# Deformable sampling on one core: where ScalarE's copy of turned samples stands in its slot

## The chip, the core and the metric

The kernel runs on one core of one Trainium2 chip. The metric is the device time of one execution in microseconds (us), the median of several. The core has TensorE (matrix products, "PE" in the profile), VectorE ("DVE"), ScalarE ("ACT"), GpSimd ("POOL"), SyncE ("SP") and DMA queues. Each engine runs its own list of instructions in order and waits on semaphores for the others.

## What is computed

Two layers work on an image of shape (4, 256, 64, 64). What matters here is layer 0. It normalizes `x` over the channels, derives 18 offsets and 9 masks for each pixel from a 3 x 3 convolution, samples the normalized image at nine shifted places for each pixel, and convolves the samples:

```python
val = ((1-wy)*(1-wx))[..., None]*corner(y0i, x0i) + ((1-wy)*wx)[..., None]*corner(y0i, x1i) \
    + (wy*(1-wx))[..., None]*corner(y1i, x0i) + (wy*wx)[..., None]*corner(y1i, x1i)
val = val * mask[..., None]
out = jnp.einsum('bkhwc,ock->bohw', val, w_conv.reshape(O, C, K))
```

Then x = x + out, and a recurrence with gates runs over the 4096 pixels of each image:

```python
i_t = sigmoid(xi_t + h @ V_i); g_t = tanh(xg_t + h @ V_c); o_t = sigmoid(xo_t + h @ V_o)
c_new = h * c + i_t * g_t
h_new = o_t * tanh(c_new)
```

Layer 1 has a gate for each channel from statistics of the whole image, and a second recurrence of the same kind.

## The kernel before, in words

The 16384 pixels lie in 128 tiles of 128 pixels by 256 channels. Each image is cut into 32 segments of 128 steps, which run beside each other on the 128 partitions; 16 warm-up steps guess each segment's start, so the first recurrence has 144 steps.

The kernel has three stretches. The first (to about 200 us) normalizes the input, writes a table of 2 x 2 pixel squares to DRAM and works out the sampling plan (`prepare`). The second, about 207 to 2290 us and the one that matters here, is `sample_and_recur` (line 577): it samples and convolves layer 0, and beside that runs the first recurrence behind the sampled tiles, and gathers the statistics for layer 1. The recurrence goes on for a short time when the sampling is done. The third is `gated_lstm`, the second recurrence.

The unit of sampling is a pair: two of the 128 x 9 combinations of tile and tap, so 576 pairs (`PAIRS`, line 601). A pair goes through six steps:

- `gather` (line 623): POOL issues two indirect DMAs, 512 KB each, that bring for each pixel its square of four corners (`squares`). There is room for five pairs.
- `scale` (line 645): ACT multiplies the first corner of each of the two by its weight and writes `v` (two activations of 128 x 256). `v` has six buffers, so three pairs.
- `combine` (line 652): DVE adds the other three corners with their weights to `v`, six instructions.
- `turn` (line 658): PE transposes the two `v` into PSUM (`tr`, two buffers).
- `copy` (line 665): ACT copies `tr` to SBUF as `vt`, one instruction of 128 x 512 (three buffers).
- `convolve` (line 672): PE multiplies `vt` with the convolution's weights and adds up in PSUM (`acc`).

The loop over slots `s` at lines 1066 to 1100 writes the order of the work out by hand, and the class `InOrder` (line 396) ties each engine's instructions to it; line 425, which the profile shows for nearly everything, is its wrapper's. In slot s the pairs stand at these steps: ACT copies pair s-2 and scales pair s+1; DVE combines pair s; PE convolves pair s-3 and, at the end of its slot, turns pair s-1; POOL gathers pair s+5. Engines run their slots independently, bound only by their waits.

A step of the recurrence comes every 4.5 slots (`step_slot`, line 926). `core` (line 987) spreads it over slots counted from `at` = 0: PE's products with h for two gates (`ga`) at 0 and for the third (`gb`) at 1; ACT's tanh and sigmoid for `tg` and `ti` at 1, `to` and `th` at 2 (`gates_of`, line 959); DVE's `cell` at 1 and `h` at 2; PE's products of the next step's input (`ga`, `gb`) at 2 and 3. Spare work (normalization, statistics, `nm`, `sq`, `xn`, `y`, `lanes`) is put behind these in each slot by `fill` (line 1047) from a list of tasks with assumed costs.

So ACT's list in slot s was: copy of pair s-2, gates if the slot has any, scaling of pair s+1, spare work.

Of the kernel before, what the change touches and what calls it, by code (L numbers as in the profile page):

```python
# [496 lines left out]
def recur(nc, G, Vs, h, shared=SHARED):  # L497

    for gs in shared:
        for g in gs:  # L500
            for m in range(NC):
                for k in range(NC):
                    nc.tensor.matmul(
                        G[g][:, m],
                        Vs[:, k, g, m * P : (m + 1) * P],
                        h[:, k],
                        start=False,
                        stop=(g == gs[-1] and m == NC - 1 and k == NC - 1),
                        skip_group_check=True,
                    )  # L510
# [30 lines left out]
def shift(nc, to, guess):  # L541

    to, guess = segments(to), segments(guess)
    nc.vector.memset(to[:, :, :, 0:1], 0.0)
    nc.vector.tensor_copy(to[:, :, :, 1:R], guess[:, :, :, 0 : R - 1])


class Spare:
# [6 lines left out]
    def give(self, engine, slot, us, do, room=lambda: True, urgent=False, soon=False):  # L555
        left = self.todo.setdefault(engine, [])
        at = 0 if urgent else sum(t[4] for t in left) if soon else len(left)
        left.insert(at, (slot, us, do, room, urgent or soon))
# [18 lines left out]
def sample_and_recur(  # L577
# [23 lines left out]
    PAIRS = NTILE * K // 2  # L601
# [43 lines left out]
    def scale(n):  # L645
        r = rounds[n]
        for i in range(2):
            v = vp.tile([P, C], F32, name="v", tag="v", bufs=6)
            nc.scalar.activation(v, r["sq"][i][:, 0:C], AF.Copy, scale=r["w"][i][0])
            r["v"].append(v)  # L650
# [43 lines left out]
    def fetch(p):  # L694

        n = 2 * p
        assert n < RING or {n - RING, n - RING + 1} <= through
        nc.sync.dma_start(place(n, 2), (x_in if n in SAMPLED else x1)[:, ORDER[n] : ORDER[n] + 2])
# [133 lines left out]
    now, free = {"slot": 0}, [*range(SQUARES)]  # L832
    taken = {"xn": 0, "y": 0, "ms": 0, "ys": 0, "cm": 0}

    def room(tag, n):
        return lambda: free if tag == "y" and now["slot"] > PAIRS + 16 else taken[tag] < n
# [89 lines left out]
    def step_slot(n):  # L926
        return START + (9 * n) // 2
# [15 lines left out]
    def project_part(n, gs):  # L943
        cm = cms[n - n % 2][:, n % 2]

        other = n % 2 and step_slot(n) > PAIRS + 8
        if gs == SHARED[0]:
            at, tag = (ps_ac, "acc") if other else (ps_a, "ga")
            ga = at.tile([P, 2, NC, P], F32, name="ga", tag=tag)
            G[n] = {gs[0]: ga[:, 0], gs[1]: ga[:, 1]}  # L950
        else:
            at, tag = (ps_tr, "tr") if other else (ps_b, "gb")
            G[n][gs[0]] = at.tile([P, NC, P], F32, name="gb", tag=tag)
        project(nc, G[n], Us, cm, (gs,))
        if gs == SHARED[1] and n % 2:
            del cms[n - 1]
            taken["cm"] -= 1

    def gates_of(n, gs):
        for g, f in gs:  # L960
            name = {2: "tg", 0: "ti", 1: "to"}[g]
            state[name] = st.tile(shape, F32, name=name, tag=name)
            for m in range(NC):
                nc.scalar.activation(state[name][:, m], G[n][g][:, m], f, bias=bs[:, g, m : m + 1])

    def added(n, slot):

        h = state.pop(("h", n))
        taken["ms"] += 1
        ht = ps_ms.tile([P, C], F32, name="ht", tag="ms")  # L970
        for k in range(NC):
            nc.tensor.transpose(ht[:, k * P : (k + 1) * P], h[:, k], ident)

        def add(slot):
            b, j = divmod(n, NB)
            plus(place(n)[:, 0], ht, b + 2, NB + j)
            taken["ms"] -= 1
            if n % 2:
                nc.sync.dma_start(x2[:, ORDER[n] - 1 : ORDER[n] + 1], place(n - 1, 2))
            if n >= LAST:  # L980
                spread(n, 1, b + 2, NB + j, slot)
            else:
                give("ACT", slot + 1, 0.9, lambda s: spread(n, 1, b + 2, NB + j, s))

        give("DVE", slot + 1, 0.48, add, urgent=n >= LAST)

    def core(s, engine):

        us = 0.0
        for n in sorted({max(0, (2 * (s - START - d)) // 9 + e) for d in range(5) for e in (0, 1)}):  # L990
            if not FIRST <= n < STEPS:
                continue
            at = s - step_slot(n)
            if engine == "PE":
                if n == FIRST and at in (-2, -1):
                    project_part(FIRST, SHARED[at + 2])
                    us += 1.8 if at == -2 else 0.9
                if at == 0 and n > FIRST:
                    recur(nc, G[n], Vs, state["h"], (SHARED[0],))
                    us += 1.8  # L1000
                if at == 1 and n > FIRST:
                    recur(nc, G[n], Vs, state["h"], (SHARED[1],))
                    us += 0.9
                if at in (2, 3) and n + 1 < STEPS:
                    project_part(n + 1, SHARED[at - 2])
                    us += 1.8 if at == 2 else 0.9
                if at == 3 and n >= WARM:
                    give("PE", s, 0.22, lambda slot, n=n: added(n, slot), room("ms", 1))
            if engine == "ACT":
                if at == 1:  # L1010
                    gates_of(n, ((2, AF.Tanh), (0, AF.Sigmoid)))
                    us += 1.0
                if at == 2:
                    gates_of(n, ((1, AF.Sigmoid),))
                    state["th"] = st.tile(shape, F32, name="th", tag="th")
                    nc.scalar.activation(state["th"], state["c"], AF.Tanh)
                    us += 0.9
            if engine == "DVE":
                if at == 1:
                    nc.vector.tensor_mul(state["tg"], state["tg"], state["ti"])  # L1020
                    nc.vector.tensor_add(state["c"], state["hc"], state["tg"])
                    us += 0.86
                if at == 2:
                    h = state["hguess"] if n == WARM - 1 else st.tile(shape, F32, name="h", tag="h", bufs=3)
                    nc.vector.tensor_mul(h, state["to"], state["th"])
                    if n >= WARM:
                        state["h", n] = h
                    if n == WARM - 1:
                        h = st.tile(shape, F32, name="h", tag="h", bufs=3)
                        shift(nc, h, state["hguess"])  # L1030
                        shift(nc, state["cell"], state["cguess"])
                        state["c"] = state["cell"]
                    state["h"] = h
                    if n + 1 < STEPS:
                        state["hc"] = st.tile(shape, F32, name="hc", tag="hc")
                        nc.vector.tensor_mul(state["hc"], h, state["c"])
                    us += 0.86
        return us
# [26 lines left out]
    s = 0  # L1065
    while s <= step_slot(STEPS) or not spare.empty():
        if s % 9 == 0 and s // 9 + 2 + FIRST // 2 <= STEPS // 2 - 1:
            p = s // 9 + 2 + FIRST // 2
            fetch(p)
            if 2 * p not in SAMPLED:  # L1070
                b, q = divmod(2 * p, NB)
                give(
                    "ACT",
                    s + 32,
                    0.9,
                    lambda slot, b=b, q=q // 2: normed(b, q, *normal[b - NTILE // NB], slot),
                    room("xn", 2),
                )
        if s > PAIRS + 16 and errands:
            errands.pop(0)(nc)  # L1080
        if 0 <= s - 2 < PAIRS:
            copy(s - 2)
        now["slot"] = s
        us = core(s, "ACT")
        if s + 1 < PAIRS:
            scale(s + 1)
        fill("ACT", s, us)
        if s < PAIRS:
            combine(s)
        fill("DVE", s, core(s, "DVE"))  # L1090
        if 0 <= s - 3 < PAIRS:
            convolve(s - 3, s)
        fill("PE", s, core(s, "PE"))
        if 0 <= s - 1 < PAIRS:
            turn(s - 1)
        if s + AHEAD < PAIRS:
            gather(s + AHEAD)
        s += 1
# [830 lines left out]
```

## Time and profile before

| | |
|---|---|
| median of 20 executions | 3220.79 us (3199.28 to 3239.57) |
| the profiled execution | 3202.81 us, of which the profile's span is 3200.9 us |
| mean granted clock of TensorE | 0.978 |
| copies `vt` from `tr`: 576, 206.8 to 2282.1 us | 336.3 us busy, 584 ns each; ACT idle ahead of them 672.4 us |
| scalings `v` from `squares`: 1152 | 527.9 us busy, 513 ns each; ACT idle ahead of them 41.2 us |
| PE in 1300 to 1600 us | 289.5 of 300 us busy |
| DVE in 1300 to 1600 us | 270.4 of 300 us busy |
| ACT in 1300 to 1600 us | 198.6 of 300 us busy |

The profile is one execution, followed by the hardware. A group is a line, an engine, an operation and the tiles that it writes and reads ("vt<-tr"). "Idle before" is the time in which the engine had nothing to run ahead of an instruction, with the engine whose release ended it. PE's starts are measured, the ends of its products modelled. In a timeline each row gives the start, the busy time, the engine, the operation, the tiles, the number of merged instructions and, in brackets, the idle time ahead and its releaser. Idle time of an engine is a loss only where the engine that sets the pace waits for it.

### The profile page before, as it was taken

What the parts mean: (1) busy time and instruction counts of PE and PEld (TensorE: products, weight loads), DVE (VectorE), ACT (ScalarE), POOL (GpSimd) and SP (SyncE); (2) the same over time, 40 slices, a digit from 0 to 9 for tenths busy, and PEclk for the clock granted to TensorE, in tenths of its full rate; (3) what the DMA queues carried; (4) which work ended last, traced back from release to release, by engine and by line L of the source; (5) the groups of instructions that cost most, each with busy time, mean ns of one, the idle gap of its engine ahead of it and who ended that gap; (6) DMA issues with size and microseconds to landing.
All of it is one profiled execution on the core that took longest, in us unless ns stands there. A gap on an engine that the chain in (4) does not pass through costs nothing.

```text
span 3200.9 us, 61683 instructions
## 1 busy us (share of the span) xinstructions
PE 3029.4 (95%) x20252; PEld 2809.6 (88%) x20252; DVE 2668.8 (83%) x7864; ACT 2043.9 (64%) x5414; POOL 1578.3 (49%) x1595
## 2 busy tenths in 40 slices
PE   7958999999999999999999999999996999999998
PEld 6947889998999889998889989999995999999997
DVE  6757778888899899998899989999777777777774
ACT  6734556666667667676676767777775666666663
POOL 3356556666666666665666656666200122222221
PEclk9979999999999999999999999999998999999999
DMA  9988788988898889998989898999401144444442
GB/s 314 326 297 332 285 287 319 329 310 317 306 334 312 310 305 331 320 322 309 330 303 329 313 318 307 333 316 327 163 27 60 60 150 151 143 151 150 150 138 87
DMA packets 319065, 822.04 MB, mean 257 GB/s; under 512 B 100872, under 2 KB 106504, under 8 KB 316432
## 3 DMA queue, kind: packets, MB, share of 16 engines
q0 software_dynamic: 189312, 672.57, 59.9%
q1 hardware_dynamic: 128992, 144.82, 13.3%
q8 instruction: 163, 2.67, 0.3%
q14 instruction: 166, 1.36, 0.1%
q10 hardware_dynamic: 432, 0.63, 0.1%
HBM read 697.98 MB, written 119.89 MB: 256 GB/s over the span
## 4 chain that ended last, share of the span: by engine, by line
PE 86%; DMA 4%; DVE 3%; ACT 3%; issue 2%; another core or an unknown queue 1%; POOL 0%; SPq 0%; ACTq 0%; DVEq 0%
PE acc L425 30%; PE ga L425 15%; PE tr L425 8%; PE gacc L425 7%; PE gtr L425 7%; PE gb L425 7%; PE gga L425 4%; PE ggb L425 4%; DMA table<-ring 2%; PE xt L425 1%; PE ht L425 1%; DMA squares<-table,used 1%; ACT v L425 1%; DMA Us<-in_L_ffn_U_c_dram 1%
## 5 line engine op out<-in xcount | busy, mean ns | idle before, releaser
L425 POOL DMA_INDIRECT squares<-table,used x1152 | 1324.1, 1149 | 755.7 <-DVE v L425 164.1
L425 DVE SCALAR_TENSOR_TENSOR v<-squares,used,v 128x256 f32<-128x256 f32 x3456 | 1413.7, 476 | 107.1 <-ACT v L425 77.7
L425 PE MATMUL acc<-wconv,vt 128*128 128x256 f32 x4608 | 1113.9, 385 | 60.5 <-ACT vt L425 38.0
L425 PEld LDWEIGHTS acc<-wconv,vt 128*128 128x128 f32 x4608 | 842.0, 193 | 166.7 <-ACT vt L425 47.2
L425 ACT COPY vt<-tr 128x512 f32<-128x512 f32 x576 | 336.3, 584 | 672.4 <-PE tr L425 529.8
L425 ACT ACTIVATE v<-squares,used 128x256 f32<-128x256 f32 x1152 | 527.9, 513 | 41.2 <-DMA squares<-table,used 36.8
L425 PE MATMUL tr<-ident,v 128*128 128x128 f32 x2304 | 350.8, 274 | 30.5 <-DVE v L425 25.4
L425 PEld LDWEIGHTS tr<-ident,v 128*128 128x128 f32 x2304 | 275.2, 142 | 42.9 <-DVE v L425 22.8
L425 PEld LDWEIGHTS ga<-cm,Us 128*128 128x128 f32 x2240 | 272.9, 193 | 8.4 <-issue 1.1
L425 PEld LDWEIGHTS ga<-h,Vs 128*128 128x128 f32 x2224 | 271.1, 193 | 6.4
L425 PE MATMUL ga<-cm,Us 128*128 128x128 f32 x2240 | 275.1, 276 | 1.4 <-issue 1.1
L425 PE MATMUL ga<-h,Vs 128*128 128x128 f32 x2224 | 273.0, 276 | 0.0
L425 DVE TENSOR_TENSOR tg<-tg,ti 128x256 f32<-128x256 f32 x280 | 118.2, 422 | 144.6 <-ACT ti L425 135.5
L425 POOL DMA_DIRECT2D hd<-sqh x60 | 35.0, 583 | 387.5 <-DVE sqh L425 325.2
L425 POOL DMA_DIRECT2D ring<-hd x240 | 144.8, 632 | 161.3 <-DMA hd<-sqh 155.1
L425 DVE TENSOR_TENSOR h<-to,th 128x256 f32<-128x256 f32 x278 | 117.1, 421 | 123.7 <-ACT th L425 119.1
L425 ACT ACTIVATE tg<-gacc,bs 128x128 f32<-128x128 f32 x280 | 87.7, 364 | 174.2 <-PE gacc L425 174.2
L425 PEld LDWEIGHTS gb<-cm,Us 128*128 128x128 f32 x1120 | 147.6, 192 | 18.0 <-issue 11.5
L425 PE MATMUL gb<-cm,Us 128*128 128x128 f32 x1120 | 152.3, 276 | 8.1 <-issue 7.7
L425 PEld LDWEIGHTS gb<-h,Vs 128*128 128x128 f32 x1112 | 145.8, 193 | 8.8 <-issue 2.4
L425 PEld LDWEIGHTS gacc<-h,Vs 128*128 128x128 f32 x1112 | 144.0, 191 | 10.0 <-DVE h L425 3.2
L425 PE MATMUL gb<-h,Vs 128*128 128x128 f32 x1112 | 148.0, 276 | 2.2 <-issue 2.2
(226 smaller groups left out, 4608.0 us busy)
## 6 DMA issues: line engine op xcount, KB each, us to landing
squares<-table,used POOLq DMA_INDIRECT x1152
ring<-in_x_dram SPq DMA_DIRECT2D x65, 256.0 KB
x1d<-ring SPq DMA_DIRECT2D x64, 256.0 KB
x2d<-ring SPq DMA_DIRECT2D x64, 256.0 KB
ring<-x2d SPq DMA_DIRECT2D x16, 1024.0 KB
out_dram<-ring SPq DMA_DIRECT2D x32, 512.0 KB
hd<-sqh POOLq DMA_DIRECT2D x60, 256.0 KB
ring<-hd POOLq DMA_DIRECT2D x240, 64.0 KB
```

Of the source, the lines that this page charges most:

```text
L425: ins = op(*args, **kw)
```

## The change

In the loop over slots, ACT now scales pair s+1 first, then works the gates if the slot has any, and then copies pair s-2; before, it copied, worked the gates and then scaled. Spare work stays last. The lists of PE, DVE, POOL and SP are the same as before.

```diff
         if s > PAIRS + 16 and errands:
             errands.pop(0)(nc)
+        now["slot"] = s
+        if s + 1 < PAIRS:
+            scale(s + 1)
+        us = core(s, "ACT")
         if 0 <= s - 2 < PAIRS:
             copy(s - 2)
-        now["slot"] = s
-        us = core(s, "ACT")
-        if s + 1 < PAIRS:
-            scale(s + 1)
         fill("ACT", s, us)
         if s < PAIRS:
             combine(s)
```

## The prediction

> **What bounds the kernel now.** I read the busy times of the whole span first. TensorE (PE) is busy 3029.4 of 3200.9 us. The sampling stretch, which the change touches, runs from the first to the last copy of turned samples, 206.8 to 2282.1 us. I then read the waits in that stretch, longest total first, and last the timeline of one stall.
>
> ```profile
> PE 3029.4 (95%) x20252; PEld 2809.6 (88%) x20252; DVE 2668.8 (83%) x7864; ACT 2043.9 (64%) x5414; POOL 1578.3 (49%) x1595
> ```
>
> ```profile
> ACT vt L425 <- PE tr L425: 529.8, 339, 7.0
> ...
> DVE v L425 <- ACT v L425: 64.3, 28, 5.1
> ...
> DVE tg L425 <- ACT ti L425: 40.1, 36, 6.3
> PE acc L425 <- ACT vt L425: 38.0, 30, 4.0
> ```
>
> The columns are total us, times, longest. ScalarE (ACT) stands idle 529.8 us ahead of its copies (vt from tr) for PE's transposes, which costs nothing by itself. What costs is the last line: 30 times PE had nothing to do until a copy was done. Those 38.0 us are the largest item of PE idle time there. From 440 to 2290 us PE's groups show 35.6 us idle ahead of the convolution (28.7 of it for copies), 8.1 ahead of gb, and 4.3 ahead of tr, ga and xt: 48.0 us in 1850. VectorE's lateness does not reach PE: "PE tr <- DVE v" is 25.4 us in two waits, 22.6 of them in one at the ramp. So PE sets the pace, and it can gain at most about 48 us here.
>
> One of the 30 waits:
>
> ```profile
> 1495.14 0.60 PE L425 MATMUL tr<-ident,v 128*128 128x128 f32 x4
> ...
> 1495.58 1.89 PE L425 MATMUL acc<-wconv,vt 128*128 128x256 f32 x8
> ...
> 1498.78 0.79 PE L425 MATMUL tr<-ident,v 128*128 128x128 f32 x4
> ...
> 1500.70 0.59 ACT L425 COPY vt<-tr 128x512 f32<-128x512 f32 x1 [6.55 <-PE tr L425]
> 1501.18 0.91 ACT L425 ACTIVATE v<-squares,used 128x256 f32<-128x256 f32 x2
> ...
> 1501.34 1.99 PE L425 MATMUL acc<-wconv,vt 128*128 128x256 f32 x8 [1.77 <-ACT vt L425]
> 1501.72 2.47 DVE L425 SCALAR_TENSOR_TENSOR v<-squares,used,v 128x256 f32<-128x256 f32 x6 [3.63 <-ACT v L425]
> ```
>
> The transposes end at 1495.74 by the trace, but ACT sees their release only at 1500.70. At once it copies; the convolution follows 0.05 us behind the copy's end, and the two scalings come behind the copy, for VectorE (DVE). The DMA share in 1495 to 1501 is 1.00 at 379 GB/s. Why the release is late I can't tell from this; what matters is what stands between it and PE. Before it is only the copy.
>
> **What the change does, part by part.** In slot s, ACT's order was copy(s-2), gates, scale(s+1), spare work. It becomes scale(s+1), gates, copy(s-2), spare work. Nothing is added or removed: 576 copies, 1152 scalings and the gate activations stay, and the lists of the other engines and queues (PE, DVE, POOL's gathers, SP's DMAs) do not change. Only one wait moves. `v` has 6 buffers, two for a slot, so scale(s+1) writes the buffers that turn(s-2) reads. Before, the copy ahead of it had waited for that turn; now each scaling carries a wait for PE itself, and the copy none. So scalings do not escape the wait on the transposes: they take it over, and gates and copy stay behind it.
>
> *What comes earlier.* (1) The scalings, by the copy, 0.48 us from its start to the next instruction's (1500.70 to 1501.18), and in the two slots of each step of the recurrence by the gates, about 1.0 us. They serve DVE, which PE does not wait for; I cost this at nothing. What hides it is PE's own queue, 97% full here. If that cover is gone, this is the faster rival below.
>
> *What comes later.* (2) The gates: they stood behind one copy (0.48 us) and now stand behind two scalings (0.66 to 0.88 us, worked out in 3), so about 0.3 us later. DVE waits 36 times for `ti`, so it may idle 36 x 0.3 = 11 us more. What hides it: PE's products with h show 0.0 us idle ahead (ga from h, 273.0 us busy). I cost it at 0; without cover it is 11.
>
> (3) The copy, by two scalings, and in 227 of 511 slots by the gates as well. A pair of scalings takes 0.91 us; the next instruction starts 0.81 to 0.88 us behind the first (1501.18 to 1501.99). The first scaling needs only the first half of the transposes, released up to 0.22 us ahead of the second. So the shift is 0.66 to 0.88 us; I take 0.75, the middle. With gates it is 1.0 more, 1.75 (tg to v in the group's rows: 1312.04 to 1313.06). Who waits for the copy: PE at convolve(s-2), in the next slot, and behind it everything on PE. Cover is the time from the copy's end to that matmul. I took it pair by pair from the trace after 440 us (the last three pairs, which have no scaling ahead, left out):
> - 39 pairs have under 0.15 us. 12 of them follow directly on another, with ACT idle for under 0.5 us, and share its shift, so 27 count once, 19 without gates and 8 with: 19 x 0.75 + 8 x 1.75 = 28 us (26 to 32 with 0.66 and 0.88).
> - Of the others without gates, 17 have 0.15 to 1.0 us (mean 0.52): those below the shift lose 5 us together. With gates, 27 have 0.15 to 1.8 us (mean 1.29): 27 x (1.75 - 1.24) = 14, less 0.05 of each cover being the semaphore's way. Together 19; but many of these are late because of a stall just before, whose shift they share. I take 10 (0 to 25).
> - The rest have cover to spare: without gates 2.7 us in the median of all, with gates 2.3, against shifts of 0.75 and 1.75.
>
> (4) The ramp, 207 to 440 us, 62 pairs. 13 of these have under 0.15 us of cover, but gathers limit there ("ACT v <- DMA squares" 20.1 us, and 22.6 us on DVE at once), and a copy behind a scaling that waits for its gather is late by that wait. Each by 0.75 would be 10 and with gates in 3 of them 13, with longer gather waits some 20, hidden 0. I take 4, nearer the hidden end, as PE is not the bound there. After the ramp gathers do not matter: no wait of ACT for a gather is listed between 700 and 2200 us.
>
> (5) The clock. After long PE waits the granted clock halves:
>
> ```profile
> 440.00:444.50 4.50, 2.97 (x8) 2.34 (x8) 2.05 (x6) 3.49 (x9) 0.00 (x0) 0.62 0.72 292
> ...
> 1915.00:1925.00 10.00, 7.70 (x34) 6.86 (x35) 6.37 (x16) 6.17 (x19) 2.15 (x2) 0.66 0.63 236
> ```
>
> The columns are stretch, us, busy time of PE, PEld, DVE, ACT, POOL, then the granted clock. At 0.62 over 4.5 us, 1.7 us of full clock are lost, at 0.66 over 10 us 3.4. Between 440 and 2290 us this happens five times (441, 820, 1342, 1762, 1916), beside PE waits of 1.5, 1.8, 3.0, 1.8 and 4.0 us; 13 waits there are of 1.5 us or more, so not each brings it. With waits 0.75 to 1.75 us longer I take two or three more such stretches: 4 us. The ends are 0 (none more) and 41 (24 stretches of 1.7 us, one for nearly every one of the 27).
>
> The Trainium skill, "TensorE: Matmul & The Clock Gate", section "HAM oscillation — how this bites in real kernels", has PE go back to the slow clock for idle gaps over about 3.4 us; by that rule waits of 1.8 + 0.75 us would bring no stretch more, term 5 would be 0 and the sum 42. The trace differs: three of the five fell beside waits of 1.5 to 1.8 us. I go by the trace.
>
> Sum: 28 + 10 + 4 + 4 = 46 us more. The profiled execution took 3202.81 us (span 3200.9 and 1.9 around it); with the change it would take some 3249. It lies 18 us under the median of the 20 runs, 3220.79, so for the median I put 3220.8 + 46 = 3267.
>
> **Rivals.**
>
> *It makes no difference (0.15).* The late releases may mostly not stand on the path: the modelled end of PE's work may hide that PE is still busy while its queue looks empty, so that a copy 0.75 us later meets a PE that was not idle. Then only the second item of term 3 is left, some 0 to 10 us, less what DVE gains: about 3224. For it: the profile gives PE's ends as modelled. Against it: a queue that is really idle is what lets the clock fall, and it falls beside these waits.
>
> *Faster (0.20).* DVE gets scaled samples 0.5 to 1.5 us earlier. DVE idles 64.3 us for `v`, 40.1 for `ti`, 34.0 for `th` in the stretch. POOL's gathers are issued on DVE's releases (164.1 us of POOL's waits), so late scalings bunch gathers, and the stall above came in a stretch of full DMA. If the late releases come of this bunching, steadier gathers would thin them out. With half of PE's 38.0 us of copy waits gone and the rest of DVE's gain hidden, that is -19: 3202. The most is -48, all PE idle. It decides if more of the 27 waits vanish than the added 0.75 or 1.75 us on those left is worth. Against it: gathers are issued some 11 us ahead of their use, and moving a scaling by 0.5 to 1.5 us in a slot of 3.5 us changes little in when DMA is full.
>
> *Much slower (0.10).* The clock falls with nearly every lengthened wait: 24 x 1.7 = 41 in place of 4, so 46 + 37 = 83, 3304. It needs waits of some 2.5 us to trigger where those of 1.7 mostly did not.
>
> *It doesn't do what it says* is no case of its own: the copies do move, and that the scalings keep a wait on PE is in the sum.
>
> **How the numbers follow.** My forecast, 3267, has 0.55. Its own range is 3247 to 3306: the low ends of the terms sum to 26; the high ends, with 8 for the clock, to 32 + 25 + 20 + 8 = 85. For 8 in 10 I reach down to 3202, which leaves out half of the faster case, and up to 3300, which leaves out half of the much slower one. Faster by over 0.2% (6.4 us, about what a measurement of this kernel can tell from no change) 0.20; within it 0.15; slower 0.65.
>
> **What would show it.** Right: "PE acc <- ACT vt" grows from 38.0 us by 30 to 50, single waits of some 1.7 become 2.4 and more; idle ahead of ACT's copies falls to nearly nothing and reappears ahead of `v` (from PE tr); DVE's waits for `v` shrink, those for `ti` grow; PE idle rises though DVE idles less in their stead. The stretch from 2290 us on keeps its length. Wrong: PE's waits for copies become fewer than 20, or stay at 1.7 with the copy still directly behind the release; or the stretch after 2290 us changes; or PE begins to wait for DVE.

## The result and the profile after

The changed kernel takes **3264.15 us** in the median of 9 runs (3250.97 to 3275.22); the kernel before, run beside it on the same chip, 3219.36 (62 runs). The ratio is 1.014, with a 95% interval of 1.0117 to 1.0164: 45 us slower. The profiled execution of the changed kernel took 3280.24 us, 16 above its median, that of the kernel before 3202.81, 17 under its own. So the two traces lie 77 us apart, the medians 45, and a size read from the traces is too large for the medians.

The busy times of the whole span, from the page of the changed kernel:

```profile
PE 3057.5 (93%) x20252; PEld 2829.2 (86%) x20252; DVE 2668.6 (81%) x7864; ACT 2046.7 (62%) x5414; POOL 1592.0 (49%) x1595
```

DVE's busy time is that of before and ACT's nearly so: nothing was added. PE's grew by 28 us in the same 20252 matmuls, so some of them ran at a lower clock.

Now the waits in the stretch of sampling, 207 to 2380 us (total us, times, longest):

```profile
ACT v L425 <- PE tr L425: 522.7, 356, 6.7
...
PE acc L425 <- ACT vt L425: 82.0, 35, 6.2
DVE tg L425 <- ACT ti L425: 75.6, 38, 6.6
...
PE tr L425 <- DVE v L425: 29.8, 2, 27.6
...
DVE v L425 <- ACT v L425: 24.0, 20, 6.5
```

The first line was "ACT vt" before, 529.8 us: the wait on PE's transposes has gone from the copy to the scaling, as large as it was. DVE's wait for `v` fell from 64.3 to 24.0, that for `ti` rose from 40.1 to 75.6. PE's wait for copies rose from 38.0 to 82.0. The groups of the page say the same of the two instructions that changed places (busy, mean ns, then the idle time ahead and the releaser of most of it). The copy before:

```profile
L425 ACT COPY vt<-tr 128x512 f32<-128x512 f32 x576 | 336.3, 584 | 672.4 <-PE tr L425 529.8
```

The scaling and the copy after:

```profile
L425 ACT ACTIVATE v<-squares,used 128x256 f32<-128x256 f32 x1152 | 529.9, 503 | 800.0 <-PE tr L425 522.7
...
L425 ACT COPY vt<-tr 128x512 f32<-128x512 f32 x576 | 331.7, 576 | 1.0 <-PE tr L425 1.0
```

The copy now hardly ever waits (672.4 us of idle time ahead of it before, 1.0 after), because the scaling ahead of it already has.

Where the time came from shows in three stretches, parted at the first copy and the last: ramp (62 pairs), rest of the sampling, tail. The columns are us, then the busy times of PE, PEld, DVE, ACT and POOL, the granted clock, DMA share and GB/s:

```profile
213.70:455.30 241.60, 204.16 (x1174) 181.87 (x1175) 177.37 (x501) 118.14 (x298) 148.25 (x127) 0.90 0.83 296
455.30:2359.80 1904.50, 1820.56 (x12068) 1686.42 (x12067) 1682.01 (x4841) 1244.77 (x3319) 1179.03 (x1014) 0.98 0.86 305
2359.80:3278.30 918.50, 870.11 (x6046) 812.36 (x6044) 676.15 (x2003) 565.60 (x1560) 180.52 (x304) 0.97 0.36 114
```

In the trace of before the same stretches take 234.2, 1841.1 and 918.8 us, with PE busy for 203.6, 1794.1 and 870.5; the middle one reads:

```profile
441.00:2282.10 1841.10, 1794.05 (x12056) 1668.34 (x12057) 1681.75 (x4840) 1241.46 (x3320) 1164.08 (x1012) 0.99 0.89 315
```

So of the 77 us, 6.9 came ahead of the first copy, in code that is the same (206.8 to 213.7 us), 7.4 in the ramp, 63.4 in the rest, and none in the tail. The 63.4 are 36.9 us more of PE idle time (47.1 to 83.9) and 26.5 us more of PE busy time in as many matmuls. The second is the clock: by the trace's records of it, five stretches of half clock before in this part, losing 10.2 us, and sixteen after, losing 35.8.

One late release in the changed kernel (start, busy time, engine, tiles):

```profile
1397.62 0.60 PE L425 MATMUL tr<-ident,v 128*128 128x128 f32 x4
...
1403.50 0.51 ACT L425 ACTIVATE v<-squares,used 128x256 f32<-128x256 f32 x1 [7.30 <-remote]
1404.91 0.51 ACT L425 ACTIVATE v<-squares,used 128x256 f32<-128x256 f32 x1 [0.90 <-remote]
1405.32 0.60 ACT L425 ACTIVATE tg<-ga,bs 128x128 f32<-128x128 f32 x2
1405.82 0.62 ACT L425 ACTIVATE ti<-ga,bs 128x128 f32<-128x128 f32 x2
1406.32 0.60 ACT L425 COPY vt<-tr 128x512 f32<-128x512 f32 x1
1406.47 0.42 DVE L425 TENSOR_TENSOR tg<-tg,ti 128x256 f32<-128x256 f32 x1 [6.55 <-ACT ti L425]
...
1406.97 2.50 PE L425 MATMUL acc<-wconv,vt 128*128 128x256 f32 x5 [5.69 <-ACT vt L425]
```

The transposes end at 1398.22, and ACT goes on only at 1403.50 and, for the second half, at 1404.91 (the profile does not name the releaser here, only "remote"). The copy starts 1.41 us behind that, after a scaling and two pairs of gates; PE stood idle for 5.69 us, in which DVE waited for the same gates. Before, the copy stood directly behind such a release. The windows view of what follows:

```profile
1404.20:1411.00 6.80, 4.03 (x11) 3.31 (x12) 4.46 (x12) 5.08 (x14) 0.93 (x1) 0.50 0.63 254
```

The granted clock is 0.50 for 6.8 us: another 3.4 us lost, seen as longer busy times and not as idle time.

### The profile page after: what moved, and what is told of

The parts are those of the page before. It is cut to its first block, busy times and chain, and to the rows that moved or that the text cites. A ratio compares the mean times of both kernels' runs of the same rounds, so it can differ in the third digit from the quotient of the medians.

```text
span 3278.3 us, 62133 instructions
## 1 busy us (share of the span) xinstructions
PE 3057.5 (93%) x20252; PEld 2829.2 (86%) x20252; DVE 2668.6 (81%) x7864; ACT 2046.7 (62%) x5414; POOL 1592.0 (49%) x1595
## 4 chain that ended last, share of the span: by engine, by line
PE 74%; issue 12%; DVE 5%; ACT 4%; another core or an unknown queue 3%; DMA 2%; POOL 0%; SPq 0%; ACTq 0%; DVEq 0%; POOLq 0%
PE acc L425 26%; PE ga L425 12%; PE tr L425 7%; PE gacc L425 6%; PE gtr L425 6%; PE gb L425 6%; PE ggb L425 3%; PE gga L425 3%; DVE v L425 3%; ACT v L425 1%; ACT vt L425 1%; PE zacc L425 1%; PE xt L425 1%; DMA table<-ring 1%
## 5 line engine op out<-in xcount | busy, mean ns | idle before, releaser
L425 POOL DMA_INDIRECT squares<-table,used x1152 | 1338.6, 1162 | 812.9 <-DVE v L425 240.3
L425 PE MATMUL acc<-wconv,vt 128*128 128x256 f32 x4608 | 1134.5, 390 | 109.8 <-ACT vt L425 82.0
L425 PEld LDWEIGHTS acc<-wconv,vt 128*128 128x128 f32 x4608 | 852.8, 195 | 225.8 <-ACT vt L425 94.0
L425 ACT ACTIVATE v<-squares,used 128x256 f32<-128x256 f32 x1152 | 529.9, 503 | 800.0 <-PE tr L425 522.7
L425 PE MATMUL ga<-cm,Us 128*128 128x128 f32 x2240 | 282.7, 278 | 8.9 <-issue 8.2
L425 PE MATMUL gacc<-h,Vs 128*128 128x128 f32 x1112 | 147.0, 275 | 1.8 <-DVE h L425 1.8
```

The costliest lines, as they stand in the source:

```text
L425: ins = op(*args, **kw)
```

## The experiments

My theory: a copy that comes later costs only where a release from PE reaches ACT late, and there PE pays for all that ACT works between release and copy, and for the clock. The rivals: the order costs by itself; the later gates cost, through DVE; the number or the length of the late releases itself changes with the order.

The kernels ran on three chips, each beside the kernel before on the same chip: its median there was 3189.44 us (the first four kernels), on the second chip 3093.05 (the next four) and in a second set 3095.60 (three more), on the third 3208.36 (the last). The chips differ by more than the change makes, and that became a finding. Of the kernel before a trace was kept on the chip of the first comparison alone, so figures of waits "before" are from there, and against traces of another chip they are a rough measure.

**Half of the change: scaling first, then copy, then gates.**

```diff
+        now["slot"] = s
+        if s + 1 < PAIRS:
+            scale(s + 1)
         if 0 <= s - 2 < PAIRS:
             copy(s - 2)
-        now["slot"] = s
         us = core(s, "ACT")
-        if s + 1 < PAIRS:
-            scale(s + 1)
```

> ACT's slot is scale(s+1), copy(s-2), gates: half of the change. Theory (what stands between the transposes' release and the copy is what PE pays): 0.75 us for every first wait and nothing for gates, so 27 x 0.75 = 20, 5 for the pairs with little cover, some 5 to 10 for ramp and clock: 30 us slower than the kernel before, ratio 1.006 to 1.012, and faster than the changed kernel. Rival (the cost is that DVE gets the gates later): here they come later still, behind scalings and copy, so at least as slow as the changed kernel, 1.014 to 1.022.

Measured: 3219.17 us, ratio 1.0086 (1.0059 to 1.0113); granted clock 0.9745 against 0.979. So the scalings alone cost some 0.9%, without the gates ahead of the copy, as the theory had it and less than the rival asked for; the full change cost 1.4% on its chip. After the ramp PE waits 34.2 us for copies (28.7 before; with the full change 48.9, and 12.3 more that the profile puts down to `ti`, the instruction just ahead of the copy).

**The gates alone: gates first, then copy, then scaling.**

```diff
+        now["slot"] = s
+        us = core(s, "ACT")
         if 0 <= s - 2 < PAIRS:
             copy(s - 2)
-        now["slot"] = s
-        us = core(s, "ACT")
         if s + 1 < PAIRS:
             scale(s + 1)
```

> ACT's slot is gates, copy(s-2), scale(s+1): only the gates are put ahead. Theory: gates do not wait for the transposes and mostly run while ACT idled for them, so the copy is late only where ACT was not idle: 0 to 10 us slower, ratio 0.998 to 1.003. Rival (gates' time for DVE decides): gates are 0.5 us and more earlier than before, so clearly faster, under 0.995.

Measured: 3174.82 us, ratio 0.9933 (0.9904 to 0.9961). **This is faster than the kernel before, and so than both orders of the change.** The theory had not expected it; the size is the rival's. Its waits from 440 to 2300 us:

```profile
ACT vt L425 <- PE tr L425: 265.1, 196, 5.9
...
DVE tg L425 <- ACT ti L425: 24.9, 23, 4.5
...
PE acc L425 <- ACT vt L425: 16.2, 18, 3.1
```

On the first chip the kernel before waited 28.7 us for copies there; but the order of before with eight buffers (below), on the same chip as this run, has 17.8, so the 16.2 here do not show where the gain comes from. What can be argued is this: the gates stand ahead of the copy here too, but they wait for PE's products of an earlier slot and not for the transposes; so they can run while ACT waits for a late release, and no longer queue up behind it. No run here takes it apart.

**More room in `v`: the changed order and the order of before, with eight buffers for six.** With eight, the scaling of pair s+1 writes buffers that an earlier turn has left, and no longer waits for the release on which the copy waits.

```diff
-            v = vp.tile([P, C], F32, name="v", tag="v", bufs=6)
+            v = vp.tile([P, C], F32, name="v", tag="v", bufs=8)
```

The changed order:

> The changed order with 8 buffers for v in place of 6, so that scale(s+1) needs turn(s-3), long done, and no longer turn(s-2). Theory: scalings and gates then run while ACT idled for the transposes, and the copy follows the release directly again except where ACT is late: between 0.990 and 1.003 of the kernel before; ACT's idle time stands ahead of the copies again. Rival (the place behind the gates costs by itself, or DVE sets the pace): 1.010 to 1.016 as in the changed kernel.

Measured: 3178.60 us, ratio 0.997 (0.9941 to 0.9998) against the kernel before. The order of before:

> The kernel before with 8 buffers for v: a control for the buffers alone. The copy ahead of each scaling has waited for the same transposes already, so both theories expect no change: 0.998 to 1.002.

Measured: 3181.15 us, 0.9972 (0.9952 to 0.9993), a little under the 0.998 expected. With eight buffers the two orders take the same time: the cost of the change hangs on the wait that the scaling takes over. The changed order's waits, 440 to 2300 us:

```profile
ACT vt L425 <- PE tr L425: 200.6, 165, 4.4
...
PE acc L425 <- ACT vt L425: 16.1, 14, 2.6
```

ACT waits ahead of its copies again, with nothing queued between release and copy. The fourth kernel's waits for copies are 17.8 us there.

**Work put ahead of each copy, or behind it.** Two copies of halves of `tr` into a tile that nobody reads, ahead of the copy (shown) or behind it:

```diff
     def copy(n):
...
+        for i in range(2):
+            junk = vp.tile([P, NC, P], F32, name="junk", tag="junk", bufs=1)
+            nc.scalar.copy(junk, r["tr"][:, i])
         nc.scalar.copy(r["vt"], r["tr"])
```

> The kernel before, with two more activations of 128x256 on ACT between the transposes' release and each copy (they copy the same transposes to a tile that nobody reads, so they wait for the release as well): 0.9 us, as long as two scalings, and nothing else is moved. Theory (PE pays for what stands between the release and the copy): 27 first waits x 0.9 = 24 us, 5 to 10 for pairs with little cover, 5 to 20 for the clock: ratio 1.010 to 1.018. Rival (what costs in the change is the scalings' own wait for the transposes, or the changed order of DVE's work): ACT has the idle time, so as the next kernel, 1.000 to 1.004.

> The same two activations directly behind each copy: the same work on ACT, scalings and gates later by 0.9 us, the copy at its old place. Theory: 1.000 to 1.005, since PE does not wait for scalings and gates. Rival: as much as with the two activations ahead.

Measured: ahead 3097.78 us, 1.0008 (0.9999 to 1.0018); behind 3095.74 us, 1.0005 (0.9996 to 1.0014). The theory's cost ahead of the copy did not come. This is the second chip, where the kernel before takes 3093 us, and what the theory needs is missing there: ACT's waits for the transposes (207 to 2300 us) are short, the longest 1.8 us against 7.0.

```profile
ACT junk L425 <- PE tr L425: 196.9, 249, 1.8
...
PE acc L425 <- ACT vt L425: 6.8, 8, 1.5
```

```profile
440.00:1000.00 560.00, 560.00 (x3826) 526.12 (x3825) 516.91 (x1499) 478.16 (x1341) 385.59 (x324) 1.00 0.92 331
1000.00:1500.00 500.00, 500.00 (x3414) 469.66 (x3412) 476.72 (x1359) 445.29 (x1238) 343.97 (x289) 1.00 0.93 332
```

In these stretches PE is busy without a gap, at the full clock, with DMA at a share of 0.92 to 0.93. So without late releases a copy 0.67 us later (the median from the first added activation to the copy) costs nothing that is clear of the noise, and a DMA share of 0.93 alone does not make releases late. Both kernels were run once more, with the next.

**The changed kernel on the second chip**, beside the padded ones.

> The changed kernel once more, on whatever chip comes, since one chip showed no late releases at all (kernel before 3093 us, PE without idle time after the ramp). Theory (the change makes late releases dearer, and costs nothing where there are none): where the kernel before takes some 3190 us or more and shows them, ratio 1.010 to 1.018 with the granted clock 0.008 to 0.010 lower; where it takes some 3093 us, 1.000 to 1.003. Rival (the order costs by itself): 1.010 or more on any chip.

> The kernel before with 0.9 us of ACT work that waits for the transposes ahead of each copy, again. Theory: with late releases on the chip 1.006 to 1.015, without them 1.000 to 1.002 as the first time. Rival (its 1.0008 held because ACT's place ahead of the copy does not matter): 1.000 to 1.002 on any chip.

> The same work behind each copy, again. Theory: with late releases 0.998 to 1.005 and clearly under the kernel with the work ahead; without them 1.000 to 1.002. Rival: no difference between the two places on any chip.

Measured: the changed kernel 3097.88 us against 3095.60, **1.0011** (1.0002 to 1.002); padded ahead 3097.13, 1.0004 (0.9995 to 1.0013); behind 3094.76, 0.9994 (0.9985 to 1.0003). Releases are not late here either: the changed kernel costs what the theory expects of such a chip, and for the padded ones theory and rival expect the same here, so they decide nothing. The changed kernel's waits from 440 to 2290 us, and its windows:

```profile
ACT v L425 <- PE tr L425: 477.6, 372, 2.6
...
DVE tg L425 <- ACT ti L425: 78.1, 59, 3.3
...
PE acc L425 <- ACT vt L425: 0.4, 2, 0.2
```

```profile
440.00:1000.00 560.00, 560.00 (x3820) 525.85 (x3820) 514.96 (x1497) 377.01 (x1019) 386.31 (x325) 1.00 0.92 331
1000.00:1500.00 500.00, 499.77 (x3415) 469.29 (x3414) 475.72 (x1361) 353.57 (x946) 343.87 (x291) 1.00 0.93 330
```

The order is the slow one, ACT's wait stands ahead of `v`, and DVE waits 78.1 us for the gates, more than on the first chip (59.8 after the ramp); yet PE idles 0.4 us for copies, and the change costs a tenth of a per cent. The rivals "the order costs by itself" and "the later gates cost, through DVE" fall: DVE's waits are there, and the time is not. On the first chip, too, none of PE's waits after the ramp is put down to DVE, before the change or after it.

**Half the gather.** Is it the DMA load that makes releases late? Each gather brings only two of the four corners, so that half of the bytes move; `combine` uses those two for all four, in the order of before and in the changed order.

```diff
-                out=sq,
+                out=sq[:, 0 : 2 * C],
...
-                nc.vector.scalar_tensor_tensor(v, sq[:, q * C : (q + 1) * C], w[q], v, ALU.mult, ALU.add)
+                nc.vector.scalar_tensor_tensor(v, sq[:, q % 2 * C : (q % 2 + 1) * C], w[q], v, ALU.mult, ALU.add)
```

> The kernel before with gathers of half the bytes: each brings the upper two corners of its squares, and VectorE takes these in place of the lower two, so the count of instructions stays and the samples are not the reference's. Theory (the releases are late where the DMA engines are full): the DMA share falls from 0.88 to about 0.5, waits for copies go from 38 us to under 10, half-clock stretches after the ramp mostly go: about 50 us less and some of the ramp, ratio 0.970 to 0.985. Rival (the late release is PE's or ACT's own): waits for copies stay near 38 us, only the ramp gains, 0.990 to 1.000.

> The changed order with the same halved gathers (lower corners replaced by the upper ones). Theory: without late releases the copy is covered in nearly all slots, so the change costs 0 to 12 us against the kernel before with halved gathers (ratio to it 1.000 to 1.004). Rival (the change's cost does not come from late releases): 30 us or more above it, ratio 1.010 or more.

Inconclusive. The whole times, 55925.8 and 55929.0 us, tell nothing, since the altered values send the kernel into a much longer branch of its own behind the sampling. The sampling stretch can be read: 1972.9 and 1971.6 us, PE idle 0.4 us after the ramp in both, DMA at some 180 GB/s. The two orders agree within 0.1%, as expected, but this was the second chip, on which releases are not late with the full gather either, so nothing follows for the DMA.

**Lateness made by hand.** So that the question does not hang on a chip: in the order of before, in every ninth slot from pair 40 on, ACT first copies `tr` eight times into a tile that nobody reads, 4.91 us. Behind that the copy comes at once, or behind the scaling (and the gates), in turn; half of the slots have gates.

```diff
+        now["slot"] = s
+        n = s - 2
+        late = 40 <= n < PAIRS - 4 and n % 9 == (4, 4, 3, 3)[n // 9 % 4]
+        last = late and n // 9 % 2 == 1
+        if late:
+            for _ in range(8):
+                junk = vp.tile([P, 2, NC, P], F32, name="junk", tag="junk", bufs=1)
+                nc.scalar.copy(junk, rounds[n]["tr"])
+        if last and s + 1 < PAIRS:
+            scale(s + 1)
-        if 0 <= s - 2 < PAIRS:
-            copy(s - 2)
-        now["slot"] = s
+        if not last and 0 <= n < PAIRS:
+            copy(n)
         us = core(s, "ACT")
-        if s + 1 < PAIRS:
+        if last:
+            copy(n)
+        elif s + 1 < PAIRS:
             scale(s + 1)
```

> Late releases made by hand, in the order of the kernel before: in every ninth slot from pair 40 on, 58 in all, ACT first copies the transposes eight times to a tile that nobody reads (some 3.9 us), so that what follows is as late as behind a late release. Four kinds take turns: a slot without gates or one with gates (to and th), and in each the copy ahead of gates and scaling, as before, or behind them, as changed. Theory: PE's wait at the convolution is longer with the copy behind by what now stands between, 0.8 to 0.9 us without gates and 1.8 to 1.9 with them, in the mean over some 14 slots of each kind; the clock halves more often after the longer ones. Rival (a late copy costs PE the same in both places, because something else of the slot is later still): differences under 0.3 us.

Measured: 3451.38 us against 3208.36, 1.0735 (1.0547 to 1.0924), all of the late slots together. What tells is the trace, four timelines of one slot each. Without gates, the copy at once and behind the scaling:

```profile
666.08 4.91 ACT L425 COPY junk<-tr 128x512 f32<-128x512 f32 x8 [0.17 <-issue]
...
670.89 0.59 ACT L425 COPY vt<-tr 128x512 f32<-128x512 f32 x1
...
671.53 0.70 PE L425 MATMUL acc<-wconv,vt 128*128 128x256 f32 x2 [2.21 <-ACT vt L425]
...
859.80 4.91 ACT L425 COPY junk<-tr 128x512 f32<-128x512 f32 x8 [1.71 <-PE tr L425]
...
864.61 0.91 ACT L425 ACTIVATE v<-squares,used 128x256 f32<-128x256 f32 x2
...
865.42 0.57 ACT L425 COPY vt<-tr 128x512 f32<-128x512 f32 x1
...
866.04 0.70 PE L425 MATMUL acc<-wconv,vt 128*128 128x256 f32 x2 [3.00 <-ACT vt L425]
```

With gates, the copy at once, and then behind scaling and gates:

```profile
1470.34 4.89 ACT L425 COPY junk<-tr 128x512 f32<-128x512 f32 x8
...
1475.12 0.59 ACT L425 COPY vt<-tr 128x512 f32<-128x512 f32 x1
...
1475.77 0.70 PE L425 MATMUL acc<-wconv,vt 128*128 128x256 f32 x2 [1.57 <-ACT vt L425]
...
2089.99 0.91 ACT L425 ACTIVATE v<-squares,used 128x256 f32<-128x256 f32 x2
2090.80 0.61 ACT L425 ACTIVATE to<-gb,bs 128x128 f32<-128x128 f32 x2
2091.30 0.42 ACT L425 ACTIVATE th<-cell 128x256 f32<-128x256 f32 x1
...
2091.61 0.59 ACT L425 COPY vt<-tr 128x512 f32<-128x512 f32 x1
...
2092.25 0.70 PE L425 MATMUL acc<-wconv,vt 128*128 128x256 f32 x2 [3.15 <-ACT vt L425]
```

PE's idle time, in brackets, goes from 2.21 to 3.00 us by a pair of scalings: 0.79. With gates it goes from 1.57 to 3.15 in the shortest case: 1.58. In the medians of 15 slots of each kind it is 2.21 and 3.00, and with gates 1.57 and 3.85. The means, on which the expectation was put, are 2.76 and 3.12, and with gates 2.04 and 3.84: 0.4 and 1.8 us apart. The first pair of means misses the 0.8 expected; two slots with the copy at once, which have waits of 5.3 and 7.1 us, raise the first of them. Where no such wait comes in, as in the slots shown, PE pays for the whole of what stands between.

The clock does not follow the length of the wait alone. In the order in which the four kinds are shown, it halved in 9 of the 15 slots of the first kind, 3 of the 15 of the second, 2 of the 15 of the third, and in all 15 of the fourth, whose waits are 3.15 us and more. The Trainium skill, "TensorE: Matmul & The Clock Gate", section "HAM oscillation — how this bites in real kernels", names gaps over about 3.4 us. Here less was enough. What decides shows in the trace's records of the granted clock: it changes only at steps of 3.41 us that run on through the whole trace. Cut at these steps (columns as above, PE's busy time first), around a wait of 2.21 us from 1264.84, and around the wait of 3.00 us that ends at 866.04:

```profile
1263.64:1267.05 3.41, 1.20 (x12) 0.96 (x11) 0.01 (x1) 3.28 (x7) 2.70 (x3) 1.00 0.50 136
1267.05:1270.47 3.42, 3.42 (x8) 2.76 (x9) 2.93 (x9) 3.36 (x11) 1.16 (x2) 0.50 0.97 351
...
860.87:864.28 3.41, 2.17 (x17) 1.85 (x16) 0.08 (x1) 3.22 (x7) 1.88 (x2) 1.00 0.86 275
864.28:867.69 3.41, 1.65 (x8) 1.47 (x9) 2.53 (x7) 3.35 (x10) 0.00 (x0) 1.00 0.71 287
867.69:871.11 3.42, 3.42 (x24) 3.14 (x23) 3.29 (x12) 2.93 (x9) 1.88 (x2) 1.00 0.40 51
```

The shorter wait lies inside one step, leaves PE 1.20 of 3.41 us busy, and the next step has half the clock. The longer one is parted over two steps, and the clock stays. In all traces but those of the halved gather, the sampling after the ramp has 6327 such steps at full clock. All 67 in which PE was busy for under 0.43 of the step were followed by half clock, none of the 6188 at 0.60 and more, and 11 of the 72 between. So what counts is PE's idle time within one step, a wait of some 2 us or several shorter ones, and where the steps fall.

The third rival, that the number or the length of the late releases changes with the order, had no run of its own. ACT's waits of over 3 us ahead of copies and scalings after the ramp are 28 before and 36 after, 24 with the scaling first and 24 in the order of before with eight buffers, but 12 with the gates first and 8 in the changed order with eight buffers. With one trace each this leaves it open as a part of the cost and of these gains; in the slots shown above, made late by hand, it has no part.

## Why the prediction was right, and which terms were not

The forecast was 3267 us with 46 more; measured were 3264 with 45. Direction and total were right, and so was the mechanism; that the total fits to 1 us is luck, for the parts do not fit so well.

- *"So scalings do not escape the wait on the transposes: they take it over"*: right. ACT idles 522.7 us ahead of `v` for the transposes and 1.0 ahead of the copies, and with eight buffers of `v`, where the scaling's wait goes, the cost goes too (0.997 and 0.9972).
- *The shift, 0.75 us and 1.75 with gates* (term 3): right; with lateness made by hand 0.79, and 1.58 in the shortest case with gates.
- *28 for the tight pairs and 10 for those with little cover* (term 3): 38 forecast; PE's idle time after the ramp grew by 36.9 us in the traces, and its waits for copies, with those put down to `ti`, by 32.5 (28.7 to 61.2). But it is not the same 27 waits: pairs with under 0.15 us of cover rose from 39 to 70, and those of them with gates from 8 to 58. PE's waits of over 0.5 us rose from 20, mean 1.61 us, to 30, mean 2.34, near the 0.75 more for each that was foretold, and of the 19 of 2 us and more (3 before) 17 are in slots with gates. In the medians, whose difference is 32 us smaller than the traces', some of the parts must be smaller; which, is not on record.
- *The ramp, 4* (term 4): 7.4 in the traces. Another 6.9 came ahead of the first copy, where the code is the same, and no term stands for that.
- *The clock, 4* (term 5): **the term that was mis-sized.** Two or three more half-clock stretches were taken; eleven more came, and 26 us in place of 4. It was sized on the five of before. The runs show why that is no measure: a step of 3.41 us has to lose over half of its PE time, and the waits of 2 us and more, which can do that by themselves, went from 3 to 19. The three waits of 1.5 to 1.8 us that brought a stretch before are near that limit, two of them with other waits in the same step. The rival "much slower" had the mechanism right in part. In the medians the term can only be bounded: the granted clock is 0.969 in the median of 11 executions and 0.978 in the trace of before, and 0.009 of 3220 us is some 29 us, an upper estimate, since that trace is 17 us faster than its kernel's median and faster executions show a higher clock (0.973 at 3250.97 us, 0.968 at 3275.22). So the clock was put too low, the other parts together are at least 16 of the 45, where 42 were forecast, and errors of opposite sign made up the total.
- *Scalings earlier, at nothing* (term 1): right. DVE's wait for `v` fell by 40 us, and no gain of it shows in PE's waits.
- *Gates later, at nothing* (term 2): right so far as the wait goes through DVE, by the chip where DVE waits 78.1 us and the time is the same. But gates have a place too: put ahead of the copy and of the scaling, they gained 0.67%, which no term had.
- *The rivals.* "No difference" is what the change does on a chip without late releases: 1.0011. The prediction took the late releases of its one trace for a property of the kernel; they came on some chips and not on another, and its case of 0.15 should have been put so. The "faster" case, that earlier scalings thin out late releases, did not come: ACT's waits of over 3 us went from 28 to 36.

What stays open: why releases come late on some chips (three were seen, and the one of the first comparison; whether it is the chip or what ran around it was not tried), since DMA was at a share of 0.93 on one without any, and the halved gather ran where it could tell nothing; how much of the cost is a different number of late releases; and why the kernels with eight buffers and with the gates first gain on the kernel before.

## What to carry to other kernels

Put nothing between the release that an in-order engine waits for and the instruction that the bounding engine needs next: what waits for that same release goes behind it, or gets a buffer more, and what waits for something earlier may run ahead, where the engine is idle anyway (the one run of that here gained 0.67%). Moving an instruction moves its wait: count the buffers to see which instruction will now carry it, and price all that stands behind. Waits of PE that add up to some 2 us within a step of 3.41 also cost clock, which shows as busy time, and a loss that rests on late events should be looked for on more than one chip before it is taken for the kernel's.

## What the runs showed of the hardware that was not expected

The same kernel takes 3093 us on one chip and 3189 to 3219 on others. On the first the longest of ACT's waits for PE's transposes after the ramp is 1.8 us, or 2.6 in the changed order, and PE hardly idles there. On the others ACT waits up to 7 us for transposes that by the trace ended long before, and the granted clock is 0.978 to 0.979 in place of 0.986 to 0.987; in the one trace of before, PE idles 47 us in that stretch. Less idle time and clock loss, the sampling after the ramp takes nearly the same: 1784 us before the change and 1785 after it on the chip of the first comparison, and 1772 on the chip without late releases.

The clock's steps are the other thing: in these traces the full clock is kept or halved every 3.41 us, by how busy PE was in the step before (under 0.43 of it, halved 67 times of 67; at 0.60 and more, never in 6188), so that a wait of 2.21 us can halve it and one of 3.00 us can leave it alone.
